# One fused opening per image: projection, norm and angles in one piece, four wide for image 0

## The chip, the cores and the metric

The kernel runs on one core of one Trainium2 chip. Its engines are TensorE (PE, matrix products), VectorE (DVE), ScalarE (ACT), GpSimd (POOL) and SyncE (SP), which issues most DMA transfers. Each engine works through its own list of instructions in order and waits for the others at semaphores. The metric is device microseconds of one execution. Before the change the median of 3 runs is 13397.82 us (13392.09 to 13401.96).

## The reference, cut to what matters

Four images of 4096 tokens with 128 channels go through two layers. The part that matters here is where the first layer ends and the second begins:

```python
y = y_f + y_b + y_s                       # three scans, each gated by silu(z)
x = x + einsum('od,bdl->blo', out_proj_w, y)       # layer 0: projection
u = layernorm(x)                          # per token, 128 channels
heads = u.reshape(B, S, 16, 8)            # S = 4096
qkv = _qz_ring(heads + rx_theta)          # cos, then products along the 8
scores = einsum('bhsd,bhtd->bhst', q, q) / sqrt(8)
ctx = softmax(scores) @ q
```

`_qz_ring` takes the cosine of the eight angles of a head and forms their running products; element 0 is the product of elements 1 to 7. After the attention follow a small feed-forward part with two more norms, and an expert layer at the end.

## The kernel before, in words

**Stages.** Everything is float32. A first stage makes the inputs of the scans for all images and runs the 384 scan steps of image 0 beside it. Then comes what the code calls the opening of image 0, then one attention loop per image (1024 rounds each: two score products and two exponents per round, and four value products), and at the end the experts. The scan steps of images 1 to 3 (`following`), the opening of the next image and the work after attention of the last one (`after`) are spread over the loops.

**Order.** Under `manual_schedule` the order of instructions on each engine is the order in which Python emits them. Every part is a generator; each `yield` is a place where another part may go on. `Pace.run(share)` adds `share` to a credit and advances the part by one yield per full credit. `flow(pieces, width, apart)` keeps up to `width` pieces going at once and starts the next when the newest has made `apart` yields. `Bank` hands out PSUM banks; a piece that finds none free yields `PE` and tries again. In the loops, `beside(i)` gives the scans of the next image 0.5 to 1.3 yields a round, and one yield, at times two, to `last` (the `after` of the image before) or, when the scans of the next image are done, to its opening. What is left of both when the loop ends runs between the loops.

**The opening of an image** has two passes over its 4096 tokens, in eight pieces of 512 tokens. First `layer` (L693), two pieces at a time: a load of x (L700), per half of the 256 inner channels four loads (L708: three scan sums `d_y` and the gate `d_sz`), three DVE operations (L713), four matmuls per PSUM bank (L721), an addition to x (L726), and a store to `t1` in DRAM (L728, on POOL's queue). Then `before` (L746), for each half of the image: `angles` (L765) for four pieces, which loads `t1` again (L769), norms it (L737, L738, the inverse root on POOL in L44 and L45, L742), stores it as `d_un` (L772), adds theta (L774) and reduces the angle to one turn (L106 to L110); one sine over all four pieces (L759, on ACT, which needs a table load, as the exponents use another table); and `rings` (L781) for four pieces: the products (L788 to L792), a copy into `v_g` and its store (L793, L794), a transpose (L797) and sixteen stores of 16 KB to `d_q` on SP's queue (L803).

**Buffers.** The pool `a_one2` has two buffers for each of x_g, p0, p1 and p2, four for y0 and one for the angles. `v_g` is one constant tile. The one PSUM bank that lies outside the loops' own pools is shared with the sums of the scan steps (L515).

**Around it.** The loop of image b first loads `qT` and `v` of its image on SP (L815, L816), makes a masked copy of 512 queries (L822), then runs scores (L833), exponents (L838) and value products (L847). There is one `qT`, so its load waits for the last scores of the loop before. A scan step is an exponent on ACT (L495) and three DVE operations (L504, L507, L509) of 1024 columns, a copy of its last column on POOL (L508), and loads of `delta` and `du` (L481) every second step.

Of the kernel before, what the change touches and what calls it, by code (L numbers as in the profile page):

```python
# [11 lines left out]
F32 = mybir.dt.float32  # L12
# [67 lines left out]

PE = "pe"


def flow(pieces, width, apart):


    pieces, active = iter(pieces), []
    more = True
    while more or active:
        if more and len(active) < width and (not active or active[-1][1] >= apart):  # L90
            piece = next(pieces, None)
            if piece is None:
                more = False
            else:
                active.append([piece, 0, None])
        for a in list(active):
            yield a[2]
            a[2] = next(a[0], a)
            if a[2] is a:
                active.remove(a)  # L100
            a[1] += 1

# [10 lines left out]
class Bank:  # L113


    def __init__(self, pool, n):
        self.pool, self.free = pool, n
# [486 lines left out]
class Attention:  # L604

    def __init__(self, tc, ctx, loop, w, gate, cols, ident, bank, dram, t1, w_out, sums, sz, x):
        nc = self.nc = tc.nc
# [26 lines left out]
        with tc.tile_pool(name="a_load", bufs=1) as load, tc.tile_pool(  # L636
# [31 lines left out]
            nc.tensor.transpose(ps[:, :E], raw, ident[:E, :E])  # L668
            nc.vector.tensor_copy(self.gate, ps[:, :E])

        self.v_g = const.tile([P, 4, VPAD], F32, name="v_g")
        nc.gpsimd.memset(self.v_g[:, :, H * VW :], 0.0)
        self.heads = self.v_g[:, :, : H * VW].rearrange("p t (h e) -> p t h e", e=VW)
        nc.gpsimd.memset(self.heads[:, :, :, D], 1.0)
        self.small = ctx.enter_context(tc.tile_pool(name="a_small", bufs=2))
        self.pieces_of(loop, 2)
# [4 lines left out]
        self.ps_o = loop.enter_context(tc.tile_pool(name="a_ps_o", bufs=1, space=PSUM))  # L681
        self.u, self.q, self.v, self.context, self.total, self.t2 = {}, {}, {}, {}, {}, {}
        self.xn, self.logits = {}, {}

    def pieces_of(self, ctx, n):

        self.one = ctx.enter_context(self.tc.tile_pool(name=f"a_one{n}", bufs=1))
        self.n, self.hidden = n, 0

    def piece(self, shape, tag, name):  # L690
        return self.one.tile(shape, F32, tag=tag, bufs=self.n, name=name)

    def layer(self, b, g):  # L693

        nc = self.nc
        xin = self.x[b].rearrange("(t p) c -> p t c", p=P)
        to = self.t1[b].rearrange("(t p) c -> p t c", p=P)
        cut = slice(g * 512, (g + 1) * 512)
        x_g = self.piece([P, 4, C], "x_g", name=f"xr_{b}_{g}")
        nc.sync.dma_start(out=x_g, in_=xin[:, g * 4 : g * 4 + 4, :])  # L700
        ys = []
        for m in range(2):
            rows = slice(m * P, (m + 1) * P)
            parts = []
            for i, src in enumerate([self.sums[b, order] for order in range(3)] + [self.sz[b]]):
                tag, bufs = ("y0", 4) if i == 0 else (f"p{i - 1}", 2)
                t = self.one.tile([P, 512], F32, tag=tag, bufs=bufs, name=f"y{i}_{b}_{g}_{m}")
                nc.sync.dma_start(out=t, in_=src[rows, cut])  # L708
                parts.append(t)
            yield  # L710
            y = parts[0]
            for t, op in zip(parts[1:], (ALU.add, ALU.add, ALU.mult)):
                nc.vector.tensor_tensor(y, y, t, op)  # L713
            ys.append(y)
        yield
        for half in range(2):
# [10 lines left out]
            self.bank.leave()  # L727
        nc.gpsimd.dma_start(out=to[:, g * 4 : g * 4 + 4, :], in_=x_g)  # L728

# [15 lines left out]

    def before(self, b):  # L746


        self.u[b] = self.dram.tile([P, NT, C], F32, name=f"d_un_{b}")
        self.v[b] = self.dram.tile([P, NT, VPAD], F32, name=f"d_v_{b}")  # L750
        self.q[b] = self.dram.tile([P, L], F32, name=f"d_q_{b}")
        for half in range(2):
            gs = range(4 * half, 4 * half + 4)
            angles = self.one.tile([P, 4, 512], F32, tag="h", bufs=self.n - 1, name=f"ang_{b}_{half}")
            yield from flow((self.angles(b, g, angles[:, g % 4, :]) for g in gs), 2, 3)
            for _ in range(4):
                yield
            nc = self.nc
            nc.scalar.activation(angles, angles, AF.Sin, bias=self.half_pi, scale=-1.0)  # L759
            yield  # L760
            yield
            yield from flow((self.rings(b, g, angles[:, g % 4, :]) for g in gs), 2, 2)

    def angles(self, b, g, a):

        nc = self.nc
        cut = slice(g * 4, g * 4 + 4)
        u = self.piece([P, 4, C], "p0", name=f"un_{b}_{g}")
        nc.sync.dma_start(out=u, in_=self.t1[b].rearrange("(t p) c -> p t c", p=P)[:, cut, :])  # L769
        yield  # L770
        yield from self.norm(u, u, f"u{b}_{g}")
        nc.gpsimd.dma_start(out=self.u[b][:, cut, :], in_=u)  # L772
        turns = self.piece([P, 4 * H, D], "p1", name=f"turn_{b}_{g}")
        nc.vector.tensor_tensor(  # L774
            a.rearrange("p (h d) -> p h d", d=D), u.rearrange("p t (h d) -> p (t h) d", d=D),
            self.theta.unsqueeze(1).to_broadcast([P, 4 * H, D]), ALU.add,
        )
        yield
        turned(nc, a, turns.rearrange("p h d -> p (h d)"))
        yield  # L780

    def rings(self, b, g, a):
        nc = self.nc
        cut = slice(g * 4, g * 4 + 4)
        a = a.rearrange("p (h d) -> p h d", d=D)
        turns = self.piece([P, 4 * H, D], "p2", name=f"ring_{b}_{g}")
        ring = turns
        nc.vector.tensor_copy(ring[:, :, 1], a[:, :, 1])  # L788
# [3 lines left out]
        nc.vector.tensor_mul(ring[:, :, 1:], ring[:, :, 1:], a[:, :, 0:1].to_broadcast([P, 4 * H, D - 1]))  # L792
        nc.vector.tensor_copy(self.heads[:, :, :, :D], ring.rearrange("p (t h) d -> p t h d", h=H))  # L793
        nc.gpsimd.dma_start(out=self.v[b][:, cut, :], in_=self.v_g)  # L794

# [480 lines left out]
def tile_kernel(tc, ctx, x, in_proj_w, dirs, out_proj_w, attn, gate, weight1, weight2, out):  # L1276
# [16 lines left out]
    with ExitStack() as fill:  # L1293
# [7 lines left out]
        with tc.manual_schedule():  # L1301
            first = Pace(scans.of_image(0, inputs.made, nc.scalar))
            others = Pace(flow(inputs.pieces(range(nb)), 2, 6))
            while not first.done:
                others.run(0.98)
                first.run(1.0)
            others.rest()
    loop = ExitStack()
    block = Attention(tc, ctx, loop, attn, gate, cols, ident, bank, dram, t1, w_out, scans.sums, inputs.sz, x)

    def opening(b):

        yield from flow((block.layer(b, g) for g in range(NT // 4)), 2, 3)
        yield from block.before(b)

    with tc.manual_schedule():
        following = Pace(*(scans.of_image(b, inputs.made) for b in range(1, nb)))
        opens = Pace(opening(0))
        while not opens.done:
            opens.run(2.0)  # L1320
            following.run(0.5)
        last = Pace()
        n = 3 * NC * NB
        for b in range(nb - 1):
            opens = Pace(opening(b + 1))

# [32 lines left out]
    with ExitStack() as end:  # L1359
        block.bank = Bank(end.enter_context(tc.tile_pool(name="end_ps", bufs=7, space=PSUM)), 7)  # L1360
        with tc.manual_schedule():
            w = {g: experts.weights(stream, g) for g in range(2)}
            with ExitStack() as pieces:
                block.pieces_of(pieces, 5)
                for _ in block.after(nb - 1):
                    pass
# [36 lines left out]
```

## Time and profile before

| what | value |
|---|---|
| median of 3 runs | 13397.82 us |
| the profiled execution | 13404.59 us |
| its span, first to last instruction | 13402.9 us |
| mean granted TensorE clock | 0.943 |
| instructions | 213892 |
| stage of scans of image 0 | 0 to 2450 us |
| opening of image 0 | 2450 to 2810 us |
| attention loops of images 0 to 3 | 2810, 5381, 8009 and 10590 to about 12960 us |

```profile
PE 12305.7 (92%) x85255; PEld 3948.9 (29%) x85255; DVE 8969.0 (67%) x8565; ACT 10704.2 (80%) x10807; POOL 3464.3 (26%) x4192
```

This line of the page has the busy time of each engine, its share of the span and its instructions. TensorE is busy for 92% of the span, but a share over the whole span is a mean over stages that are limited by different things; each stage has to be read by itself. The costliest groups of the page belong to the loops and to the scans:

```profile
L838 ACT ACTIVATE e<-s 128x1024 f32<-128x1024 f32 x8192 | 7905.3, 1027 | 1026.3 <-PE s L833 847.4
L833 PE MATMUL s<-qm,qT 32*128 32x512 f32 x32768 | 5416.6, 642 | 127.9 <-DVE qm L822 76.3
L507 DVE TENSOR_TENSOR_SCAN h<-dA,ends,dB 128x1024 f32<-128x1024 f32 x576 | 1374.5, 2386 | 197.9 <-ACT dA L495 140.9
```

A row names line, engine, operation, output and inputs with their shapes and the count; after the first bar stand the busy time in us and the mean of one in ns, after the second the idle time of the engine just before them and what ended most of it. A matmul counts twice here[...].

In the time-ordered view a row has its start, its length, engine, line and operation, and in brackets how long the engine had stood idle before it and what it waited for. A name such as `SPq` stands for the issuing of DMA transfers by SP.

### The profile page before, as it was taken

The page shows a single profiled execution, that of the slowest core. Times are in us where ns is not written, and L with a number is a line of the kernel's source. Part 1 is how long each engine was busy: PE and PEld are TensorE (multiplying, and loading weights), DVE is VectorE, ACT ScalarE, POOL GpSimd, SP SyncE. Part 2 cuts the span into 40 slices and gives each one's busy share as a digit, 9 for nine tenths or more (in the row PEclk, how much of TensorE's full clock was granted, in tenths as well). Part 3 has the DMA queues.
Part 4 walks back from the last instruction along what each step waited for, and adds up shares of the span by engine and source line. Part 5 has one row for each costly group of instructions (what it writes and reads, how often), then busy time and mean ns, then how long its engine had stood idle before and what let it go on. Part 6 is the DMA issues. An engine that isn't in the chain of part 4 may idle for free. (4 is left out here: it accounts for less than half of the span.)

```text
span 13402.9 us, 213892 instructions
## 1 busy us (share of the span) xinstructions
PE 12305.7 (92%) x85255; PEld 3948.9 (29%) x85255; DVE 8969.0 (67%) x8565; ACT 10704.2 (80%) x10807; POOL 3464.3 (26%) x4192
## 2 busy tenths in 40 slices
PE   7797978369999999999999999999999999999976
PEld 3232333112222222233332222333323222222224
DVE  6998989678888877888888679888884210000014
ACT  5665656269999998899999889999998888888851
POOL 2333334222333322223333223333331000000001
PEclk8887988679999999999999999999999999999986
DMA  5666666544444444544444545444443100000015
GB/s 143 185 181 178 193 176 194 154 121 120 117 120 113 107 127 120 142 112 116 111 112 112 130 126 130 107 115 114 110 113 98 51 19 9 9 7 30 12 36 178
DMA packets 703778, 1490.44 MB, mean 111 GB/s; under 512 B 185406, under 2 KB 318838, under 8 KB 702774
## 3 DMA queue, kind: packets, MB, share of 16 engines
q1 hardware_dynamic: 512078, 1057.83, 30.6%
q0 software_dynamic: 139584, 300.84, 7.2%
q10 hardware_dynamic: 51112, 118.08, 3.3%
q8 instruction: 667, 10.93, 0.3%
q14 instruction: 337, 2.76, 0.1%
HBM read 1167.22 MB, written 308.94 MB: 110 GB/s over the span
## 5 line engine op out<-in xcount | busy, mean ns | idle before, releaser
L838 ACT ACTIVATE e<-s 128x1024 f32<-128x1024 f32 x8192 | 7905.3, 1027 | 1026.3 <-PE s L833 847.4
L833 PE MATMUL s<-qm,qT 32*128 32x512 f32 x32768 | 5416.6, 642 | 127.9 <-DVE qm L822 76.3
L847 PE MATMUL acc<-e,v 128*32 128x512 f32 x32768 | 4387.5, 607 | 25.1 <-ACT av L856 22.1
L508 POOL COPY ends<-h 128x1 f32<-128x1 f32 x1536 | 1841.9, 1199 | 5104.7 <-DVE h L507 5088.8
L833 PEld LDWEIGHTS s<-qm,qT 32*128 32x128 f32 x32768 | 1790.0, 183 | 3288.8 <-PE s L833 1438.0
L847 PEld LDWEIGHTS acc<-e,v 128*32 128x32 f32 x32768 | 647.0, 108 | 3163.7 <-issue 3027.8
L507 DVE TENSOR_TENSOR_SCAN h<-dA,ends,dB 128x1024 f32<-128x1024 f32 x576 | 1374.5, 2386 | 197.9 <-ACT dA L495 140.9
L507 DVE TENSOR_TENSOR_SCAN h<-delta,ends,du 128x1024 f32<-128x1024 f32 x576 | 1354.1, 2351 | 164.7 <-ACT delta L495 95.5
L495 ACT ACTIVATE dA<-delta,A 128x1024 f32<-128x1024 f32 x768 | 886.8, 1155 | 339.6 <-DMA delta<-d_delta 217.7
L504 DVE TENSOR_TENSOR dB<-du,B 128x1024 f32<-128x1024 f32 x768 | 935.2, 1218 | 211.8 <-PE y L515 193.1
L495 ACT ACTIVATE delta<-delta,A 128x1024 f32<-128x1024 f32 x768 | 886.6, 1154 | 179.4 <-PE y L515 168.8
L509 DVE TENSOR_TENSOR du<-h,C 128x1024 f32<-128x1024 f32 x768 | 940.7, 1225 | 26.3
L509 DVE TENSOR_TENSOR dB<-h,C 128x1024 f32<-128x1024 f32 x768 | 940.7, 1225 | 26.3
L504 DVE TENSOR_TENSOR du<-du,B 128x1024 f32<-128x1024 f32 x768 | 934.2, 1216 | 0.0
L862 POOL DMA_DIRECT2D d_ctx<-av x512 | 262.2, 520 | 1615.9 <-ACT av L856 1609.4
L515 PE MATMUL y<-dB,sel 128*32 128x256 f32 x6144 | 498.1, 397 | 124.3 <-DVE o L531 109.3
L361 PE MATMUL cv<-xn,conv 128*128 128x512 f32 x1024 | 492.4, 640 | 40.7 <-DVE xn L298 18.4
L515 PE MATMUL y<-du,sel 128*32 128x256 f32 x6144 | 494.2, 395 | 25.3 <-DVE du L509 25.3
L507 DVE TENSOR_TENSOR_SCAN h<-dA,dB 128x1024 f32<-128x1024 f32 x192 | 446.9, 2328 | 54.1 <-ACT dA L495 32.1
L507 DVE TENSOR_TENSOR_SCAN h<-delta,du 128x1024 f32<-128x1024 f32 x192 | 440.1, 2292 | 43.1 <-ACT delta L495 18.7
L531 DVE SCALAR_TENSOR_TENSOR o<-us,D,y 128x256 f32<-128x256 f32 x384 | 206.1, 537 | 353.3 <-PE y L515 353.1
L414 PE MATMUL sp<-s,minus 128*128 128x512 f32 x384 | 222.4, 663 | 207.7 <-ACT s L408 207.7
(248 smaller groups left out, 7676.3 us busy)
## 6 DMA issues: line engine op xcount, KB each, us to landing
delta<-d_delta SPq DMA_DIRECT2D x768, 512.0 KB
du<-d_du SPq DMA_DIRECT2D x576, 512.0 KB
du<-d_du ACTq DMA_DIRECT2D x192, 512.0 KB
d_u<-u POOLq DMA_DIRECT2D x48, 1024.0 KB, 5.6
B<-d_bc SPq DMA_DIRECT2D x96, 512.0 KB
C<-d_bc SPq DMA_DIRECT2D x96, 512.0 KB
d_delta<-r POOLq DMA_DIRECT2D x48, 1024.0 KB, 5.4
d_du<-u POOLq DMA_DIRECT2D x48, 1024.0 KB, 6.6
```

What stands on the lines that cost most here:

```text
L361: nc.tensor.matmul(ps[:, cut], w["conv"][:, k, m * P : (m + 1) * P], reads(k, g), start=(k == 0), stop=(k == 3))
L414: nc.tensor.matmul(ps[:, cut], sign, t[:, m, cut], start=(i == 0), stop=(i == 2))
L495: nc.scalar.activation(tiles["delta", s], t, AF.Exp, scale=A)
L504: nc.vector.tensor_mul(dB, du, spread[order, c, "B", j % 2])
L507: nc.vector.tensor_tensor_scan(h, dA, dB, first, ALU.mult, ALU.add)
L508: nc.gpsimd.tensor_copy(ends[order, c][:, at : at + 1], h[:, T - 1 :])
L509: nc.vector.tensor_mul(dB, h, spread[order, c, "C", j % 2])
L515: nc.tensor.matmul(y[32 * g : 32 * g + 32, : T // 4], self.sel[:, j // 2, :], hC[:, 256 * g : 256 * g + 256], start=(j == 0), stop=(j == 3),)
L833: nc.tensor.matmul(s_ps[:, k, :], qT[at : at + 32, kc * P : (kc + 1) * P], queries[j, qb][at : at + 32, :], start=True, stop=True,)
L838: nc.scalar.activation(e, s_ps, AF.Exp, scale=1.0 / math.sqrt(D))
L847: nc.tensor.matmul(accs[j, qb][32 * k : 32 * k + 32, :], v[:, kc, h * VW : h * VW + 32], es[i][k // 2][:, k % 2, :], start=(kc == 0), stop ...
L862: nc.gpsimd.dma_start(out=self.context[b][h * D : h * D + D, cut], in_=av[32 * k : 32 * k + D, :])
```

## The change: what it does

1. **One piece for both passes.** `layer` and `angles` become `tokens`: the normed tokens are computed from `x_g`, which is still in SBUF, and not loaded again from `t1`. The store to `t1` stays. `heads` holds the sine and the rings of a half image. It yields the new mark `WAIT` until four pieces of its half have their angles; `flow` doesn't count such yields for `apart`.
2. **Image 0 four wide.** Its opening has a pool of its own, `a_one4`: four buffers for x_g, the normed tokens (t1) and turns or rings (x1), eight for y0, six each for p0 to p2, three for the angles. It also has six PSUM banks of its own. All ten parts (four pieces, `heads`, four pieces, `heads`) go through one `flow` of width 4. The loops' pools and banks are opened only afterwards, in `begin`.
3. **Images 1 to 3** keep width 2 and the pool `a_one2`; the second half begins when the rings of the first are done.
4. **Pace.** During the opening of image 0 the ratio of opening yields to scan yields goes from 2.0 : 0.5 to 1.0 : 0.15.
5. **Two `v_g`** per pool in place of one constant tile, each with its two memsets.

```diff
-            a[1] += 1
+            a[1] += a[2] is not WAIT
...
+    def pieces_of(self, ctx, n, ahead=2, opening=True):
+        nc, self.ahead = self.nc, ahead
         self.one = ctx.enter_context(self.tc.tile_pool(name=f"a_one{n}", bufs=1))
         self.n, self.hidden = n, 0
+        self.values = []
+        for i in range(2 if opening else 0):
+            v_g = self.one.tile([P, 4, VPAD], F32, tag=f"v_g{i}", name=f"v_g{n}_{i}")
...
-    def layer(self, b, g):
+    def tokens(self, b, g, angles):
...
-                tag, bufs = ("y0", 4) if i == 0 else (f"p{i - 1}", 2)
+                tag, bufs = ("y0", 2 * self.n) if i == 0 else (f"p{i - 1}", self.ahead)
...
-        nc.gpsimd.dma_start(out=to[:, g * 4 : g * 4 + 4, :], in_=x_g)
+        nc.gpsimd.dma_start(out=to[:, tiles, :], in_=x_g)
+        u = self.piece([P, 4, C], "t1", name=f"un_{b}_{g}")
+        yield from self.norm(u, x_g, f"u{b}_{g}")
+        nc.gpsimd.dma_start(out=self.u[b][:, tiles, :], in_=u)
+        a = angles[:, g % 4, :]
+        nc.vector.tensor_tensor(
+            a.rearrange("p (h d) -> p h d", d=D), u.rearrange("p t (h d) -> p (t h) d", d=D),
+            self.theta.unsqueeze(1).to_broadcast([P, 4 * H, D]), ALU.add,
+        )
+        yield
+        turns = self.piece([P, 4 * H, D], "x1", name=f"turn_{b}_{g}")
+        turned(nc, a, turns.rearrange("p h d -> p (h d)"))
+        self.angled[b] += 1
+        yield
...
-    def before(self, b):
+    def opening(self, b):
...
-            yield from flow((self.angles(b, g, angles[:, g % 4, :]) for g in gs), 2, 3)
-            for _ in range(4):
-                yield
-            nc.scalar.activation(angles, angles, AF.Sin, bias=self.half_pi, scale=-1.0)
...
+            parts.append([self.tokens(b, 4 * half + g, angles[half]) for g in range(4)] + [self.heads(b, half, angles[half])])
+            if self.n == 2:
+                yield from flow(parts.pop(), 2, 3)
+        yield from flow((piece for part in parts for piece in part), self.n, 3)
+
+    def heads(self, b, half, angles):
+        while self.angled[b] < 4 * half + 4:
+            yield WAIT
+        for _ in range(4 if self.n == 2 else 1):
+            yield
+        self.nc.scalar.activation(angles, angles, AF.Sin, bias=self.half_pi, scale=-1.0)
...
-    def angles(self, b, g, a):
-        u = self.piece([P, 4, C], "p0", name=f"un_{b}_{g}")
-        nc.sync.dma_start(out=u, in_=self.t1[b].rearrange("(t p) c -> p t c", p=P)[:, cut, :])
...
-        turns = self.piece([P, 4 * H, D], "p2", name=f"ring_{b}_{g}")
+        v_g, values = self.values[g % 2]
+        ring = self.piece([P, 4 * H, D], "x1", name=f"ring_{b}_{g}")
...
+    with ExitStack() as wide:
+        block.pieces_of(wide, 4, 6)
+        block.bank = Bank(wide.enter_context(tc.tile_pool(name="o_bank", bufs=6, space=PSUM)), 6)
+        with tc.manual_schedule():
+            opens = Pace(block.opening(0))
+            while not opens.done:
+                opens.run(1.0)
+                following.run(0.15)
+    block.bank = bank
     loop = ExitStack()
...
-        while not opens.done:
-            opens.run(2.0)
-            following.run(0.5)
```

## The prediction

> **What bounds the kernel now.** I read the 40 slices of the span first, then busy time by windows of 250 us, then the waits and the time-ordered view of the one stretch that stood out.
>
> ```profile
> PE   7797978369999999999999999999999999999976
> ACT  5665656269999998899999889999998888888851
> ```
>
> From slice 9 on, TensorE is busy in nine tenths of almost every slice: these are the four attention loops. Before lies the scan stage of image 0, and between the two one slice where TensorE and ScalarE drop to 3 and 2. That is the opening of image 0 (about 2450 to 2810 us), which no loop covers. In windows:
>
> ```profile
> 2470.00:2766.00 296.00, 48.26 (x254) 33.33 (x254) 180.60 (x302) 31.00 (x26) 50.19 (x56) 0.52 0.48 133
> 2766.00:2810.00 44.00, 0.00 (x0) 0.00 (x0) 24.60 (x53) 2.25 (x2) 5.63 (x8) 0.50 0.41 100
> 2810.00:5381.00 2571.00, 2536.76 (x19744) 730.74 (x19744) 2092.09 (x1648) 2380.62 (x2491) 778.60 (x899) 0.99 0.47 119
> 5381.00:8030.00 2649.00, 2587.54 (x20188) 778.18 (x20189) 2156.80 (x2051) 2397.25 (x2489) 815.34 (x955) 0.99 0.47 120
> ```
>
> The columns after the length are busy us of PE, weight loads, DVE, ACT and POOL. In the opening every microsecond is on the path: loop 0 starts when it ends. DVE leads with 180.6 of 296 us, so the other 115 are waits of DVE; the waits view of that stretch names them (us in total, times, longest):
>
> ```profile
> DVE y L713 <- DMA y<-d_y: 68.6, 14, 22.2
> DVE st_u L737 <- DMA un<-t: 15.9, 1, 15.9
> DVE xr L726 <- PE out L721: 14.8, 7, 2.2
> DVE un L742 <- POOL rs_u L45: 8.6, 6, 1.4
> ```
>
> In loops 0 and 1 TensorE is idle only 34 and 61 us; there the later openings run beside it. The time-ordered view shows the idle places, all on or beside L759 and L815:
>
> ```profile
> 5321.95 2.00 ACT L759 ACTIVATE ang<-ang,a_half_pi 128x2048 f32<-128x2048 f32 x1 [9.44 <-DVE ang L110]
> ...
> 5381.43 5.33 PE L833 MATMUL s<-qm,qT 32*128 32x512 f32 x16 [10.30 <-DVE qm L822]
> ...
> 7949.28 2.00 ACT L759 ACTIVATE ang<-ang,a_half_pi 128x2048 f32<-128x2048 f32 x1 [9.75 <-DVE ang L110]
> ...
> 8008.67 5.32 PE L833 MATMUL s<-qm,qT 32*128 32x512 f32 x16 [9.75 <-DVE qm L822]
> ...
> 10589.96 1.99 PE L833 MATMUL s<-qm,qT 32*128 32x512 f32 x12 [0.40 <-DVE qm L822]
> ```
>
> ScalarE stands still for 9 to 10 us before a sine, since DVE is late with its angles, and TensorE stands 10 us at the start of loops 1 and 2, but only 0.40 us at loop 3.
>
> **The opening of image 0, to the first ring of half 1.** From the first y sum after the last scan rows have landed (2473.1) to 2766.1 it takes 293 us now.
>
> *Work of DVE.* The fusion keeps every DVE instruction: eight pieces of projection, norm and angles, and four rings. Only scan steps of image 1 leave, since their share falls from 0.5 per two opening steps to 0.15 per one. The instruction lists of the two programs put 17 scan steps ahead of this ring before and 9 after. One step (L504, L507, L509) takes 4.79 us from start to start. 180.6 - 8 x 4.79 = 142 us.
>
> *Waits of DVE.* (a) The 22.2 us wait: four B/C and four delta/du loads of 0.5 MB are issued ahead of piece 1's second half, and the window 2475 to 2500 runs at 247 GB/s with a DMA share of 0.99. They stay in the list: kept, 22. (b) The other y waits, 68.6 + 2.6 (for d_sz) - 22.2 = 49: a piece's loads are issued only when the sums of the piece before free p0 to p2 (two buffers), then land 5 us later. Six buffers let them go three pieces ahead, as long as SP is free. But SP now also carries, between the loads of pieces 4 to 7, the ring stores of half 0: sixteen at 0.5 us stand ahead of piece 5's loads, which cannot go before ring 0 is transposed; DVE has 8 us of sums and ring 1 meanwhile against 15 for issue and landing. I leave 7 there, and 13 for landings beside other traffic: 20. At best 0, at worst all 49. (c) The reload of t1 (un<-t) goes with its 15.9: 0. What is late next there is the y sums, counted in (b). (d) xr<-PE: one PSUM bank made DVE and PE take turns of 2.2 us; with six banks the matmuls of both halves run ahead: 2, at worst 14.8. (e) un<-POOL stays: in the list the norm of pieces 2, 3, 5 and 7 follows its statistics with nothing between: 8. POOL's t1 store (0.76 us) now stands ahead of each rsqrt: with gaps, 4.
>
> Sum: 142 + 22 + 20 + 2 + 8 + 4 = 198 against 293, **-95** (ends: -125 with 26 of waits, -52 with all of b and d kept).
>
> *Two weights.* The Trainium skill's "Perfetto Trace Analysis", section Optimization Strategy, says that where the most contended engine changes between regimes, interleaving them may help; that speaks against taking scan steps out of a stage with idle PE and ACT. By the rule the nine steps (43 us of DVE) belong here. By the rows they cost far less in the loop: 403 rounds with 177 steps take 1000 us (L838 and L495 counts, 3000 to 4000), 2.481 us a round, and 431 rounds without steps 2.320 (11000 to 12000); 0.161 / 0.439 = 0.37 us a step. Row: 9 x 0.37 = **+3** in loop 0 (at most 9 x 1.15 of ACT = 10) against -38 in the sum above; the rule would turn the sign, so the row is taken. Second, can DMA become the bound? To that ring the stage moves 18.9 MB of x and y, 6.6 of stores and 8.8 for scans, 34 MB. At the 247 GB/s of the row that is 139 us, at the 341 GB/s that "DMA: Bandwidth & Descriptors", section Bandwidth, gives for 1 MB loads 101 us (an estimate). Both lie under 198; the row leaves less room, and I use it.
>
> **The tail to loop 0** (44.4 us) is bound by SP: 64 ring stores of half 1 in 15.68 + 18.57 us, then qT. The list has the same 64 in a row, with two scan loads ahead and three behind. qT, v and the new pool's four memsets now lie on memory of the wide pool, so they wait for its last stores (v lands in 2.7 us): +1 (0 to 3). Memsets cost under 1 us each on a POOL 17% busy and have only `ends` copies behind them.
>
> **Openings of images 1 to 3, in the loops.** Two wide as before, the same DVE work, eight reloads less each; all scan steps still fall in the same loops (counts at loop starts differ by one).
>
> *Loop starts.* Before, the last q stores of 0.5 us stand on SP ahead of the new qT load at loops 1 and 2 (8 of them from 5371.3, after the last scores had ended at 5367). At loop 3 the opening was done in time: 0.40. In the new list the second sine comes 15 rounds earlier in both loops and five scan loads stand between the last stores and qT. So 10.30 and 9.75 fall to about 0.4: **-19** (at worst -5).
>
> *Sines.* Both 9.4 and 9.8 us come from an un<-t load 20 us late behind the q stores (DVE waits of 19.6 and 20.6 in these loops), followed by four dense angle pieces. The wait moves to piece 4's y sums, as these loads now stand behind the same stores; TensorE was 49.98 of 50 us busy over that wait, so ACT has that much cover. But now 70 rounds lie between it and the sine instead of 40, so DVE has caught up. Half credit: **-10** (-19 to +10).
>
> *After(b)* behind the loop start is emitted 15 to 32 rounds denser; its stretches now idle TensorE some 15 us per loop (5400 to 5700). **+4** (-5 to +15).
>
> **Total**: -95 + 1 + 3 - 19 - 10 + 4 = -116. The profiled execution took 13404.6 us (span 13402.9), 7 above the median of 13397.8; the difference carries over: 13397.8 - 116 = **13282**. The ends do not all meet; as independent half widths (36, 4, 7, 15, 10) they make 41, so 13241 to 13323 for this case.
>
> **Rivals.**
>
> 1. *Loads stay late in the opening* (SP's stores between the loads, or DMA pace): (b) and (d) kept, -52 in place of -95: 13325. For: DMA share is already 0.54 in 2500 to 2633, and SP's order is strict. Against: the waits of (b) come 1 to 9 us at a time, each after a buffer came free.
> 2. *The loops give nothing*: 0 for starts and sines, after(b) +15, steps +10: -69, 13329. For: the interleaving shifts everywhere. Against: the 0.40 at loop 3.
> 3. *Slower.* In loops 0 and 1 each of 16 fused pieces holds DVE on late y loads as long as un<-t does today (20.6). A piece passes every 25 us with DVE idle 35% (4950 to 5150), 8.8 us of cover; beyond it the exponents of the scans stop on ACT, and the loop with them. 16 x (20.6 - 8.8) = 189; with -91 for opening and steps: about 13496. It decides from 8.8 + 91/16 = 14.5 us a piece. Against: today's y waits in these loops are 3.3 us at most, with the same two buffers.
> 4. *No effect*: the wide pool waits for the scan stage's memory, or the loop pools for the wide one, and the gain is lost: within 27 us of before. Against: all is landed by 2470, before the first y can come.
> 5. *Everything at its good end*: -157, 13241 or less.
>
> Chances: forecast 0.72, rivals 1 to 5: 0.11, 0.07, 0.03, 0.03, 0.04. A difference under 0.2% (27 us) can't be told from none. Faster 0.94, same 0.03, slower 0.03. The range takes in rivals 1 and 2 and the good end: 13236 to 13340.
>
> **What would show it.** Loop 0's first score near 2715 (right) or after 2755 (rival 1); DVE waits for y near 40 in the opening, un<-t gone; first scores of loops 1 and 2 with under 2 us of idle; sines with under 5; TensorE idle in loops 0 and 1 near 20 and 45. Wrong if DVE waits for y over 10 us recur in the loops (rival 3), or if the opening shrinks and loop 0 grows by more than 10.

## The result, and the profile after

The changed kernel takes 13287.09 us (median of four runs, 13276.74 to 13291.25) against 13399.89 us for the kernel before on the same chip: a ratio of 0.9915, with a 95% interval of 0.9898 to 0.9932. That is 112.8 us less; the forecast was 116 less. The same kernel, run again on another chip (e10_after below), was 136.1 less than the kernel before there. The profiled execution of the changed kernel took 13276.74 us, with a span of 13275.0.

The page of the changed kernel, its busy totals and two rows of the 40 slices:

```profile
PE 12311.7 (93%) x85255; PEld 3959.8 (30%) x85255; DVE 8963.1 (68%) x8565; ACT 10702.1 (81%) x10807; POOL 3471.0 (26%) x4198
...
PE   7797879489999999999999999999999999999976
...
ACT  5665756289999998999999989999998888888851
```

The totals are as before to 0.3%: no engine has lost work. The one low slice of TensorE is still there, but a 4 has taken the place of the 3. The change is in waits, so it is read by windows. A row has the window, its length, the busy us of PE, weight loads, DVE, ACT and POOL, and then clock, DMA share and GB/s. The five rows are the opening up to the first ring of half 1, the tail to loop 0, then loops 0, 1 and 2.

```profile
2471.30:2657.20 185.90, 37.20 (x190) 29.72 (x190) 140.42 (x276) 21.92 (x18) 39.29 (x46) 0.55 0.60 173
2657.20:2703.80 46.60, 0.01 (x2) 0.04 (x2) 20.20 (x50) 0.99 (x1) 4.12 (x10) 0.50 0.45 113
2703.80:5259.10 2555.30, 2540.48 (x19808) 733.48 (x19808) 2128.29 (x1674) 2387.20 (x2498) 788.53 (x905) 1.00 0.48 120
5259.10:7865.50 2606.40, 2564.51 (x20050) 771.19 (x20049) 2147.66 (x2046) 2382.13 (x2473) 822.34 (x953) 0.99 0.47 118
7865.50:10455.00 2589.50, 2542.68 (x19766) 763.54 (x19768) 1957.40 (x1917) 2343.76 (x2433) 762.69 (x905) 0.99 0.42 108
```

The opening took 293 us and takes 186. DVE was busy for 181 of 296 us and is busy for 140 of 186. The waits of DVE in that stretch (us in total, times, longest):

```profile
DVE y L723 <- DMA y<-d_y: 38.5, 5, 18.1
DVE un L765 <- POOL rs_u L45: 6.1, 5, 1.6
DVE y L723 <- DMA y<-d_sz: 1.8, 3, 0.9
DVE h L508 <- DVE dB L505: 0.5, 1, 0.5
```

The wait for the reload of `t1` (15.9) and the seven for the projection (14.8) are gone, and those for `d_y` fell from 68.6 us in 14 to 38.5 in 5. (Both lists hold a wait of 7 us that ended just as the stretch began.) In the loops, the time-ordered view of a sine and of the starts of loops 1 and 3:

```profile
5173.58 1.28 ACT L790 ACT_TABLE_LOAD   x1
5174.87 2.00 ACT L790 ACTIVATE ang<-ang,a_half_pi 128x2048 f32<-128x2048 f32 x1
```

```profile
5259.14 1.99 PE L846 MATMUL s<-qm,qT 32*128 32x512 f32 x12
...
10454.84 1.99 PE L846 MATMUL s<-qm,qT 32*128 32x512 f32 x12 [0.51 <-DVE qm L835]
```

No bracket means no idle time before it: ScalarE runs straight into the sine, where it stood for 9.44 us, and loop 1 starts without the 10.30 us.

Where the span's 127.9 us went: scans of image 0 -1.8, opening -107.1, tail +2.0, loop 0 -15.5, loop 1 -21.0, loop 2 +8.3, everything from loop 3 on +7.3. The last can't be put down to the change: over all profiles of this study that remainder lies between 2808.8 and 2823.0, before at 2813.5. The profiled execution before was 5 us above its median in this comparison and that of the changed kernel 10 below, which is the 15 between -127.9 and -112.8.

### The profile page after: what moved, and what is told of

Read it like the earlier page. It is cut to its first block, busy times and chain, and to the rows that moved or that the text cites. A ratio compares the mean times of both kernels' runs of the same rounds, so it can differ in the third digit from the quotient of the medians.

```text
span 13275.0 us, 213812 instructions
## 1 busy us (share of the span) xinstructions
PE 12311.7 (93%) x85255; PEld 3959.8 (30%) x85255; DVE 8963.1 (68%) x8565; ACT 10702.1 (81%) x10807; POOL 3471.0 (26%) x4198
## 5 line engine op out<-in xcount | busy, mean ns | idle before, releaser
L516 PE MATMUL y<-dB,sel 128*32 128x256 f32 x6144 | 496.0, 396 | 16.4 <-DVE o L532 16.4
L516 PE MATMUL y<-du,sel 128*32 128x256 f32 x6144 | 492.0, 393 | 6.1 <-DVE du L510 6.1
```

What stands on the lines that cost most here:

```text
L516: nc.tensor.matmul(y[32 * g : 32 * g + 32, : T // 4], self.sel[:, j // 2, :], hC[:, 256 * g : 256 * g + 256], start=(j == 0), stop=(j == 3),)
```

## The experiments

All stages in one table, in us. "Stretch" goes from the first y sum after the last scan rows to the first ring of half 1, "tail" on to the first masked queries, and the loops from masked queries to masked queries. The ratio is to the kernel before on the same chip.

| kernel | stretch | tail | loop 0 | loop 1 | loop 2 | median | ratio |
|---|---|---|---|---|---|---|---|
| before | 293.0 | 43.8 | 2570.9 | 2627.2 | 2581.3 | 13399.89 | 1 |
| the change | 185.9 | 45.8 | 2555.4 | 2606.2 | 2589.6 | 13287.09 | 0.9915 [0.9898, 0.9932] |
| e1_narrow | 232.5 | 42.6 | 2557.3 | 2603.1 | 2579.3 | 13309.39 | 0.9926 [0.9913, 0.9940] |
| e2_buf2 | 186.8 | 45.8 | 2554.6 | 2610.8 | 2588.5 | 13282.62 | 0.9905 [0.9892, 0.9919] |
| e3_bank1 | 191.4 | 46.9 | 2559.2 | 2607.6 | 2594.7 | 13293.50 | 0.9916 [0.9902, 0.9929] |
| e8_both | 191.2 | 47.2 | 2561.6 | 2610.3 | 2592.9 | 13291.98 | 0.9915 [0.9900, 0.9930] |
| e4_noscan | 129.1 | 40.5 | 2578.9 | 2610.3 | 2587.8 | 13237.34 | 0.9873 [0.9859, 0.9886] |
| e7_late | 133.2 | 49.7 | 2562.6 | 2599.3 | 2581.2 | 13227.90 | 0.9867 [0.9850, 0.9883] |
| e6_actq | 182.9 | 35.9 | 2554.6 | 2609.9 | 2588.7 | 13267.86 | 0.9897 [0.9883, 0.9912] |
| e5_oldloops | 185.5 | 45.8 | 2574.9 | 2616.1 | 2581.1 | 13294.99 | 0.9917 [0.9903, 0.9932] |
| e9_best | 130.1 | 41.5 | 2560.3 | 2597.8 | 2584.4 | 13206.04 | 0.9850 [0.9835, 0.9864] |
| e10_after | 186.6 | 47.0 | 2553.5 | 2610.9 | 2594.6 | 13272.36 | 0.9898 [0.9881, 0.9914] |
| e11_spread | 184.4 | 43.7 | 2562.0 | 2604.5 | 2581.6 | 13267.22 | 0.9897 [0.9880, 0.9913] |
| e12_dense | 179.1 | 40.0 | 2557.4 | 2607.0 | 2592.3 | 13265.81 | 0.9898 [0.9883, 0.9912] |

How fine is this table? The change itself ran twice: stretch and tail repeat to 1.2 us, a loop to 5, and the median to 15 (the ratio to 0.0017). So the stages decide, and the medians only where they differ by more. Each stage was measured in one profile of each kernel.

### What shortened the opening: fusion, width, buffers or banks

**Fusion alone** (two pieces wide, two buffers, the shared bank):

```diff
-    with ExitStack() as wide:
-        block.pieces_of(wide, 4, 6)
-        block.bank = Bank(wide.enter_context(tc.tile_pool(name="o_bank", bufs=6, space=PSUM)), 6)
-        with tc.manual_schedule():
...
     block.begin(loop)
     with tc.manual_schedule():
+        opens = Pace(block.opening(0))
+        while not opens.done:
+            opens.run(1.0)
+            following.run(0.15)
```

> The fusion alone: image 0's opening in the fused form, but as narrow as those of the other images (two pieces wide, two buffers for each load, the bank shared with the scan sums), scan share 0.15 as in the change. The list has 12 scan steps ahead of the first ring of half 1 (change 9, before 17). My theory (the width, the buffers and the banks carry a good part): from before only the reload's wait of 15.9 us and five scan steps (24 us) leave, so from the first y sum to that ring about 250 us (before 293.0, change 185.9), y waits of DVE near 65 and waits for the projection near 15; time about 13287 + 64 = 13350. Rival (the fused order is what gained, width and banks are idle): under 210 us in that stretch, time under 13315.

The stretch lies between the two, and on the theory's side: 232.5 us. The time, 13309.39, lies on the rival's side (under 13315): loops 1 and 2 are 13.4 us shorter than the change's, for a reason that the section on the loops gives. Its waits of DVE in the opening:

```profile
DVE y L723 <- DMA y<-d_y: 54.4, 11, 20.1
DVE xr L736 <- PE out L731: 8.7, 4, 2.2
...
DVE ring L801 <- ACT ang L790: 3.5, 1, 3.5
...
DVE un L765 <- DMA t<-xr: 1.4, 1, 1.4
```

From before to here 60.5 us leave: the reload's 15.9, five scan steps (24), 14 of y waits (68.6 to 54.4) and 6 of waits for the projection. From here to the change another 46.6 leave: three scan steps (14), 16 of y waits, 8.7 of the projection, and the 3.5 and 1.4 of the last two lines; these make 44 of it.

Width is not all that sets this kernel apart from the wide ones. At two wide the second half of the image begins only when the rings of the first are done; at four wide both halves share one `flow`. The longest wait of e1_narrow, 20.1, stands just there. SP issues all 64 ring stores of half 0 before the first loads of half 1 (those go out from 2604.3), and DVE waits for these:

```profile
2568.82 16.80 SPq L816 DMA_DIRECT2D d_q<-ang  x32
...
2586.97 17.27 SPq L816 DMA_DIRECT2D d_q<-ang  x32
```

```profile
2610.16 1.42 DVE L723 TENSOR_TENSOR y<-y,y 128x512 f32<-128x512 f32 x2 [20.11 <-DMA y<-d_y]
```

In the change, DVE's wait behind ring stores is half as long:

```profile
2579.88 1.44 DVE L723 TENSOR_TENSOR y<-y,y 128x512 f32<-128x512 f32 x2 [9.95 <-DMA y<-d_y]
```

No run changed the width alone, with the halves kept apart.

**Two buffers, one bank, and both**, each at four wide:

```diff
-        block.pieces_of(wide, 4, 6)
+        block.pieces_of(wide, 4, 2)
```

> As the change, four wide and with its own six banks, but two buffers for each of the three y loads in place of six. Theory: the buffers let the loads run ahead; without them the y waits of DVE in the opening go from 38.5 back towards 65, the stretch to the first ring of half 1 from 186 to about 213, time about 13314. Rival (the loads are bound by SP's order and the DMA engines, not by buffers): y waits stay within 5 us of 38.5 and the time within 8 us of 13287.

```diff
-        block.bank = Bank(wide.enter_context(tc.tile_pool(name="o_bank", bufs=6, space=PSUM)), 6)
```

> As the change, four wide and with six buffers, but the one bank that is shared with the scan sums in place of six of its own. Theory: DVE and TensorE take turns at the bank again, waits of DVE for the projection near 15 us in place of 0 to 2, stretch to the first ring of half 1 about 199, time about 13300. Rival (four pieces give DVE enough other work between two turns at the bank): the waits stay under 4 us, time within 5 us of 13287.

> As the change, four pieces wide, but with two buffers for each of the y loads and the shared bank, both at once. Each alone left the stretch to the first ring of half 1 at 186.8 and 191.3 us (change 185.9). Theory (the width alone carries the difference between 232 two wide and 186 four wide): 187 to 196 us, y waits of DVE near 40, waits for the projection under 4, time within 10 of the change. Rival (buffers and banks stand in for one another, either hides the lack of the other): 210 us or more, time 20 or more above the change.

The line that was to move, first with two buffers, then with one bank:

```profile
DVE y L723 <- DMA y<-d_y: 39.3, 4, 19.4
```

```profile
DVE xr L736 <- PE out L731: 2.2, 1, 2.2
```

My theory on the buffers falls: with two, DVE waits for y as with six (39.3 against 38.5), and the stretch is 186.8. One bank costs 5 us rather than 13; 2.2 of them are the wait for the bank and 2.1 one for the sine. Both together cost 5.3, so neither hides the lack of the other. What is left between e8_both (191.2) and e1_narrow (232.5) is the order: four pieces in turn, so that between two steps of one piece lie steps of three others and DVE has work while a load lands or TensorE fills a bank, and both halves in one flow. (e8_both also keeps the wide pool's other buffers: eight for y0, four each for x_g, t1 and x1, three for the angles.) How the 41 us divide among these is not shown. The six buffers add nothing that these runs can tell, and the six banks 5 us.

A likely reason why buffers don't help stands in the first 51 us of the stretch (DMA share and GB/s are the last two numbers), with six buffers and with two:

```profile
2471.30:2522.30 51.00, 12.42 (x48) 10.68 (x48) 27.79 (x52) 5.74 (x5) 8.88 (x8) 0.50 1.05 300
```

```profile
2480.50:2531.50 51.00, 12.42 (x48) 10.68 (x48) 26.56 (x52) 5.30 (x5) 8.87 (x8) 0.50 0.96 261
```

The DMA engines are busy throughout either way (a share over 1 comes from counting a transfer where it starts), and the longest wait, 18.1 and 19.4 us, stands in this window. The next, about 10 us in both, is behind the ring stores on SP. More buffers shorten neither. e2_buf2's median is 4.5 below the change's: no difference that these runs can tell.

### Scan steps in the opening

```diff
-                following.run(0.15)
+                following.run(0.0)
```

> As the change, but no scan step at all in the opening of image 0 (share 0 in place of 0.15): ten steps and their loads move into loop 0. By the rows of the profile (4.79 us of DVE a step in the opening, 0.37 a step in the loop): the stretch to the first ring of half 1 falls from 185.9 by 9 x 4.79 = 43 and by about 12 of the first y wait (the scan loads no longer stand ahead of y), to about 131; the tail loses about 5 (two scan loads ahead of qT); loop 0 grows by 4; time about 13287 - 56 = 13231. By the rule that regimes are to be interleaved: the steps cost in loop 0 what they cost in the opening, loop 0 grows by some 40, and the time stays within 15 of 13287.

The stretch fell to 129.1 as worked out (131), the tail to 40.5. Loop 0 did not grow by 4 but by 23.5. Its first 100 us, and the waits there that matter:

```profile
2648.70:2748.70 100.00, 91.12 (x636) 25.15 (x640) 75.43 (x52) 81.96 (x86) 21.28 (x19) 0.89 0.67 175
```

```profile
DVE dB L505 <- DMA du<-d_du: 22.3, 1, 22.3
...
ACT dA L496 <- DMA delta<-d_delta: 9.1, 2, 6.9
PE s L846 <- ACT e L851: 8.6, 2, 7.8
```

The scan's first loads now stand behind qT and v. ScalarE takes its instructions in order: it stands at the scan's exponent for `delta`, the exponents of the scores stand behind it, and TensorE loses 8.6 us. Its 636 products take 6.3 us more than at the change's rate (99.74 us for 748), under a clock of 0.89 against 0.95. Third, the steps' sums on TensorE (L516) are busy for 219.8 us in loop 0 against 216.5, with the sums of eight more steps: 0.42 us a step, near the row's price of 0.37. These make 18.2 of the 23.5; 5.3 are not assigned, about what a loop repeats to. So the start cost most of it and the steps little. To test that, the scans come back once the last piece's angles are done:

```diff
-                following.run(0.15)
+                following.run(0.0 if block.angled.get(0, 0) < 8 else 0.5)
```

> As the run without scan steps in the opening, but from the last piece's angles on the scans get a share of 0.5: their first loads go out behind the last y load and ahead of the ring stores of half 1, one step stands ahead of the first ring of half 1 and four in the tail, where DVE waits 24.5 us for qT and v. In the run without steps loop 0 was 23 us longer (2578.9 against 2555.4), of which its profile shows 8.6 of TensorE waiting for the first scan loads and a clock of 0.89 in the first 100 us. Theory (that is a start-up price, not a price of ten steps): stretch about 135, tail 46, loop 0 about 2558, together 2739 against 2787 of the change and 2748 of the run without steps; time about 48 below the change. Rival (steps cost 2.3 us each in the loop, wherever the loads stand): loop 0 near 2567, together 2748, no better than without steps.

The first 100 us of its loop 0:

```profile
2670.00:2770.00 100.00, 99.57 (x748) 28.57 (x752) 86.25 (x60) 89.33 (x94) 27.80 (x27) 0.94 0.56 151
```

TensorE is full again: 748 products, 112 more than without steps. Loop 0 is 2562.6, midway between the theory (2558) and the rival (2567); that the start is the cause is shown by these 100 us, where 15 of the 16 us lie. Stretch, tail and loop 0 make 2745.5, where 2739 was worked out, against 2748.5 without steps. Loop 0 has its start back (16 us less than without steps), but stretch and tail paid 13 of it: they are 4 and 9 longer, since the early loads and five steps now stand there. The 3 us that remain are less than a loop repeats to, so placing the loads early is no gain that these runs can tell. The median is 9.4 below e4_noscan's, on another chip; in the profiles loops 1 and 2 make more than that (5180.5 against 5198.1), for the reason given below. Most of the gain over the change comes from the steps that left the opening, not from where the loads went.

### The tail

```diff
             for k in range(4):
-                nc.sync.dma_start(out=to[i, k], in_=rows[k])
+                queue = nc.scalar if self.n == 4 and i % 2 else nc.sync
+                queue.dma_start(out=to[i, k], in_=rows[k])
```

> As the change, but in image 0's opening every second group of four q stores (i = 1 and 3) is issued on ScalarE's queue in place of SP's. Theory: SP's issue of about half a microsecond a store is what the tail waits for, and what holds the y loads of pieces 5 to 7: the tail (first ring of half 1 to the first masked queries, 45.8 us) loses about 8, the stretch before it (185.9) about 6, time about 14 below the change. Rival (the tail is bound by DVE's rings and by the landing of the last stores, whoever issues them): tail and stretch stay within 3 us, and a store waiting on ScalarE holds up exponents of the scan steps: time the same or up to 10 above.

The queue of SP in the tail, first of the change, then of this run (start, us, queue, what it issues):

```profile
2661.35 31.00 SPq L816 DMA_DIRECT2D d_q<-ang  x64
...
2694.63 0.34 SPq L828 DMA_DIRECT2D qT<-d_q  x1
```

```profile
2664.08 21.06 SPq L817 DMA_DIRECT2D d_q<-ang  x32
...
2687.44 0.34 SPq L829 DMA_DIRECT2D qT<-d_q  x1
```

In the change the 64 stores pass in 31 us, 0.48 each, and qT goes out 37.4 us after the first ring of half 1; here after 27.5 (the first ring is at 2659.9). The tail is 35.9 instead of 45.8: SP's issue was its bound, as I had put it. The stretch before it lost 3 rather than 6. ScalarE paid with 16.61 us between two scan exponents in the tail, in which it issued its stores and nobody needed it.

**Both gains together**, beside the change on the same chip:

> Both gains together: half of image 0's q stores on ScalarE's queue, and the scans kept out of the opening until the last piece's angles. Theory (the two act on different terms, DVE work with early loads, and SP's issue in the tail): stretch about 130, tail about 39, loop 0 about 2562; time about 12 under the run with late scans, some 60 under the change. Rival (with steps and stores both in the tail, stores on ScalarE's queue hold up the exponents of the four steps, or the tail is bound by the landing of qT and v): tail stays near 50, time within 4 us of the run with late scans.

> The change once more, unaltered, on the chip of the run that joins both gains, as its measure: stretch within 3 us of 185.9, tail within 2 of 45.8, loops 0 to 2 within 6 of 2555, 2606 and 2590; time about 0.9915 of before. If one of these lies farther off, what the other runs show of that stage is no finer than that.

e9_best takes 13206.04 us against 13272.36: 66 us less than the change, with intervals of the ratio that do not touch (0.9835 to 0.9864, and 0.9881 to 0.9914). The tail is 41.5, 8 shorter than with late scans alone. Of the 22 us between its median and that of e7_late, the stages up to loop 1's end explain 15. But the 66 us are not the two gains alone: loops 1 and 2 are 23 us shorter than in e10_after, by the placing of the work after attention, which is read next. It is the fastest kernel of the study.

### The openings in the loops

The old two passes for images 1 to 3 only (the old functions stand beside the new ones again):

```diff
+    def layer(self, b, g):
...
         self.angled[b] = 0
+        if self.n == 2:
+            yield from flow((self.layer(b, g) for g in range(NT // 4)), 2, 3)
+            yield from self.second_pass(b)
+            return
         angles, parts = [], []
```

> Image 0 opened as in the change; images 1 to 3, inside the loops, opened in the old two passes (projection and store, then reload, norm and angles, then rings). Theory: the shorter loops 0 and 1 of the change (2555 and 2606 us, before 2571 and 2627) come from the fused openings that run beside them; with the old ones loop 0 is back at about 2571, loop 1 at 2627, with the idle of TensorE of about 10 us at the starts of loops 1 and 2 and of ScalarE of about 9 at two sines, and loop 2 falls from 2590 back to 2581: time about 28 above the change. Rival (the loops moved for another reason, by where image 0's opening leaves the scans): loops stay within 4 us of 2555 and 2606 and the time within 8 of the change.

The old waits come back in their places, at the start of loop 1 and at a sine (the lines are numbered anew in this kernel; L944 holds the scores, L799 the sine):

```profile
5281.24 5.33 PE L944 MATMUL s<-qm,qT 32*128 32x512 f32 x16 [8.30 <-DVE qm L933]
```

```profile
5223.24 2.00 ACT L799 ACTIVATE ang<-ang,a_half_pi 128x2048 f32<-128x2048 f32 x1 [9.29 <-DVE ang L111]
```

Loop 0 is back at 2575 (+19) and loop 2 at 2581; loop 1 got 10 of the 21, and what keeps it 11 under before, with the old openings and the old stalls, is not shown. The three loops make 7772 against 7751 and 7759 in the two profiles of the change. The medians (8 above the first, 23 above the second run of the change, on other chips) confirm no more than the sign.

Why was loop 2 longer after the change? The instruction lists differ in one respect: the first pass of the work after attention is emitted in rounds 8 to 82 of loop 2, where before it had 8 to 114. This hangs on the credits that the opening of image 0 leaves. A share of 0.13 in place of 0.15 there spreads the pass over rounds 9 to 109; a share of 0.14, with as many steps ahead, keeps it dense:

> The change with a scan share of 0.13 in image 0's opening (9 steps ahead of loop 0 in place of 10). Through the credits this also moves where the work after attention is emitted in the next loops: the first pass of it spreads over rounds 9 to 109 of loops 1 and 2, where the change has rounds 9 to 92 and 8 to 82. Theory (the density of that pass is what loop 2 lost and what loop 1 did not gain): loop 1 about 2600 and loop 2 about 2581, against 2606 to 2611 and 2590 to 2595 in the two runs of the change; stretch about 181; time about 20 below its partner with share 0.14. Rival (loop lengths scatter by this much, density has no part): loops 1 and 2 within 4 us of the partner's.

> The partner: share 0.14, the same 9 steps ahead of loop 0 (8 ahead of the first ring of half 1), but the first pass after attention in rounds 9 to 92 of loop 1 and 8 to 82 of loop 2, as in the change. Theory (density): loop 1 about 2608, loop 2 about 2590, stretch about 181, time about 5 below the change and 20 above the partner. Rival (scatter): as the partner within 4 us a loop.

Loop 2 answers (2581.6 against 2592.3), loop 1 hardly (2.5, within the scatter). The first 200 us of loop 2, spread and then dense:

```profile
7878.40:7978.40 100.00, 83.69 (x614) 24.73 (x616) 72.57 (x74) 73.02 (x76) 22.92 (x25) 0.90 0.61 166
7978.40:8078.40 100.00, 99.13 (x788) 29.83 (x780) 96.17 (x102) 94.05 (x100) 36.59 (x40) 1.00 0.58 150
```

```profile
7860.80:7960.80 100.00, 81.25 (x610) 24.93 (x612) 72.65 (x79) 71.92 (x75) 23.53 (x26) 0.90 0.61 169
7960.80:8060.80 100.00, 94.97 (x744) 29.25 (x742) 94.28 (x125) 87.29 (x91) 33.24 (x35) 0.97 0.53 142
```

TensorE is busy for 182.8 of these 200 us spread and 176.2 dense: 6.6 of the 10.7 us lie here. As times the two runs are equal (13267.22 and 13265.81): opening and tail, where the two shares place the steps differently, took back 9 us and loop 0 another 5. So between these two kernels the whole gains nothing.

The other kernels of the table confirm it, and for loop 1 too. Read from their traces, the first pass lies spread (rounds 10 to 110 of loops 1 and 2) in e1_narrow, e7_late, e9_best and e11_spread, and dense as in the change in the other eight with fused openings. Loop 2 takes 2579.3 to 2584.4 us in the four and 2587.8 to 2594.7 in the eight, loop 1 2597.8 to 2604.5 and 2606.2 to 2610.9; the means differ by 9.5 and 7.9. The kernels differ in their openings as well, so for loop 1 this is a sign and not a proof. It also means that e1_narrow, e7_late and e9_best owe some 17 us of their times to this placing, and not to what their edits were meant to test.

Both first hundreds are low, at 81 to 84 us busy, and so is the change's (82.70), where before had 95.12 just after its stall:

```profile
8008.70:8108.70 100.00, 95.12 (x712) 28.79 (x712) 80.89 (x85) 83.05 (x87) 26.42 (x28) 0.93 0.57 163
```

```profile
7865.50:7965.50 100.00, 82.70 (x622) 24.93 (x620) 72.83 (x79) 72.88 (x76) 23.56 (x26) 0.90 0.59 167
```

The change's time-ordered view of the start of loop 2, ScalarE and then TensorE:

```profile
7886.77 1.15 ACT L496 ACTIVATE dA<-delta,A 128x1024 f32<-128x1024 f32 x1 [9.05 <-DMA delta<-d_delta]
```

```profile
7888.89 2.08 PE L846 MATMUL s<-qm,qT 32*128 32x512 f32 x4 [8.21 <-ACT e L851]
...
7907.72 1.22 PE L944 MATMUL co<-w_comb,cT 128*128 128x128 f32 x4 [8.76 <-DVE o L532]
```

The stall at the start has moved. The first scores go at once, but the scan's next `delta` load stands on SP behind the sixteen loads of qT and v; from 12 to 21 us into the loop ScalarE stands for it, and TensorE behind ScalarE, as in e4_noscan's loop 0. The second wait is another: it ends with DVE, which had stood 23.6 us for the load of `sum` (13.9 before), issued on SP behind that `delta`. That the fused openings brought these waits to loop 2 is shown by e5_oldloops: with the old stall of 9.4 back there, TensorE waits only 3.3 us in the 100 us after it. Putting the `delta` load ahead of qT in loops 1 and 2 was not tried; what it would win there stays open.

## Why the prediction was right, point by point

**Opening, -95: measured -107.** Term by term in the stretch of 185.9: DVE work 142, measured 140.4. (a) The wait behind the first scan loads 22, measured 18.1; e4_noscan, without those loads, waits 0.5 us at this place, and 14.5 for y in the whole stretch against 31.3, so they make some 17 of it. (b) Other y waits 20: the list of 40.3 holds one of 7.2 that ended as the stretch began, so 40.3 - 18.1 - 7.2 = 15.0, of which 9.95 stand at piece 5 behind the ring stores, where I had left 7. (c) 0, measured 0. (d) 2, measured 0. (e) and gaps 12, measured 6.6 + 5.8 = 12.4. The size was right, the reason of (b) and (d) was not: I gave (b) to six buffers and (d) to six banks. e2_buf2 and e3_bank1 show that two buffers do as well and that one bank costs 5 us; what carries these terms is the order on DVE, four pieces in turn and both halves in one flow. The 49 us from which (b) started were 42: one wait of 7.3 ended as the stretch began. On the second weight, the DMA: over the stretch its share is 0.60, at 173 GB/s, so it is not the bound of the whole; in the first 51 us it has no room (above). The 247 GB/s that I took for its pace is no limit: 300 GB/s passed in those 51 us.

**Tail, +1: +2.0.** Its bound, the issue of 64 stores on SP, is shown by e6_actq. I had not seen that halving it was worth 10 us.

**Scan steps, +3 in loop 0.** The price of 0.37 us a step holds as 0.42 of TensorE. The weight of row against rule was right in sign and large in size: taking the last steps out too gains 62 in stretch and tail and loses 23.5 in loop 0. But the rule of interleaving regimes that the prediction weighs has something in it that my row could not show: a stream of scans also has a start, and a start inside a full loop is paid by TensorE (8.6 us of wait).

**Loop starts, -19, and sines, -10.** Both idle times went completely: 10.30 and 9.75 to nothing, 9.44 and 9.75 to nothing. Of the sines' idle time all 19 went, where I took half; what each was worth to a loop was not measured apart, but TensorE's idle time fell by about one start and one sine in each of loops 0 and 1 (34 to 15, 61 to 42). The starts gave 20 at the place I named, but in the first 100 us after it TensorE now waits 8.9 us in loop 1 (5.6 before, the stall apart) and 17.3 in loop 2 (4.9 before). That takes back 16 of the 20: net 4, where I forecast 19. I named the wait that goes; I did not ask what is late next on SP, which are the scan's `delta` and `sum` behind qT.

**After(b), +4.** The dense pass costs loops 1 and 2 together 13 us by e11_spread and e12_dense, and 17 by the means over twelve kernels. That is at or past the end of +15: the reason was right, the size was not.

**The loops in sum**: 3 - 19 - 10 + 4 = -22 was predicted. Before, loops 0 to 2 took 7779.4; the four profiles with the change's own order in the loops (the change twice, e2_buf2, e6_actq) have 7751.2, 7759.0, 7753.9 and 7753.2, a mean of 7754.3: -25. That the sum was right is luck. With the sizes measured here the terms make 3 - 4 - 19 + 13 to 17 = -7 to -3; some 20 us come from something that I had no term for. Part of it lies in loop 2 after its first 200 us, where TensorE idles 29.8 us before, 29.7 in e5_oldloops and 21.3 in e11_spread: the fused opening of image 3 loads it better, though no start or sine stalled there. The rest stays open.

**The total.** That 116 and 112.8 lie 3 us apart is luck as well: the second run of the change has 136.1, the opening gave 12 more than forecast, and the stages after loop 2 moved by 7 on their own. What the runs bear out is the direction, the opening as the main term, and the range.

**The rivals.** 1 (loads late): the y waits of the opening did not stay, 15 us are left of 42. 2 (loops give nothing): -25. 3 (slower, from 14.5 us of y wait a piece in the loops): in the fused opening beside loop 0 (4800 to 5259) DVE waits for y

```profile
DVE y L723 <- DMA y<-d_y: 9.3, 4, 7.2
```

four times in all, 7.2 at most; beside loop 1 it waits 9.4 us, 8.8 at most. 4 (no effect) and 5 (all at the good end, 13241) are excluded by 13287. Of the signs named beforehand, loop 0's first score came at 2703.8 (2715 named), TensorE idles 15 and 42 us in loops 0 and 1 (20 and 45 named), and loop 0 shrank.

## What to carry to other kernels

In a stage that nothing covers, count the waits of the busiest engine and give it more pieces to turn to, before giving it more buffers: four pieces in flight, with both halves in one flow, did what six buffers and six banks were meant to do, and two buffers and one bank were within 5 us of them. Look first whether the DMA engines have room: here they were busy throughout where DVE waited longest, and more buffers gained nothing. Work of a later stage that shares that engine belongs where it is hidden (4.8 us of DVE a step in the opening, 0.4 of TensorE in the loop); a stream that starts inside a full loop pays for its start there (16 us here), and starting it earlier cost 13 ahead of the loop. And when a stall at a start is removed, read the next 100 us on the same queue: what stood behind the stalled load is now the late one. A change of a pace in one stage can also move work in a later one: compare where that work lies before a gain is put down to the edit.

## What was not expected of the hardware

The small stores of the tail are bound by their issue: 64 stores of 16 KB take 31.0 us on one queue, 0.48 each, while the DMA share of that window is 0.45; halved between two queues, they shortened the tail by 9.9 us, though 32 of them still took 21.1 us on SP. And a wait of ScalarE for one load stops all exponents behind it: 9.05 us for `delta` became 8.21 of TensorE.
